# Two attention layers on one core: layer 0's weight pairs folded into one matrix each

The kernel runs on one core of a Trainium2 chip. The metric is the device time of one execution in microseconds; lower is better.

## The reference, cut to what matters

```python
# layer 0, 8 images of 1024 tokens, 256 channels, 4 heads, float32
qkv = einsum('bnc,cd->bnd', xf, W_qkv)            # q, k, v of each head: 256 wide
atten = softmax(einsum('bihd,bjhd->bijh', q, k) * C ** -0.5, axis=2)
res = einsum('bijh,bjhd->bihd', atten, v)
x1 = einsum('bnd,dc->bnc', res.reshape(B, -1, h * C), W_out) + b_out + xf
# layer 1: one head, keys 32 wide
b = softmax(einsum('bik,bjk->bij', x1 @ Wg + bg, x1 @ Wf + bf), axis=-1)
y = gamma * einsum('bij,bjd->bid', b, x1 @ Wh + bh) + x1
```

Per head, q k^T = x (Wq Wk^T) x^T, and (p v) Wo = p (x (Wv Wo)). Each bracket is a 256x256 product that doesn't depend on the image.

## The kernel before

```python
class Layer0:
    def prepare(self):                      # once per image and head
        for dst, col0 in ((self.q, 0), (self.k, C)):
            project_T(dst, w, col0, C, xT, ...)          # q^T and k^T, 16 instructions each
        project_rows(self.v, w, 2 * C, xT, ...)
    def rhs(self, c, k):
        return self.k[:, c, ts(k, NB)]
    def values(self, blk, pT):              # once per block of four query tiles
        for d in range(CC):
            ...                             # pav: 8 products of 128x512 over the keys
            nc.scalar.copy(res[:, d, :], pm)
        return lambda: self.project_out(blk, res)        # runs one step later
    def project_out(self, blk, res):
        for c in range(CC):
            ...                             # po: 2 products of 128x512 with W_out
            nc.vector.tensor_tensor(acc, pm, acc, ALU.add)   # acc: layer 0's output x1T

def scores(a, n, t):                        # one query tile
    ...                                     # s = q k^T, 128x1024 in PSUM
    nc.vector.tensor_reduce(nmax, s, AX.X, ALU.max, negate=True)
    if a.scale != 1.0:
        nc.vector.tensor_scalar(nbias, nmax, a.scale, None, ALU.mult)
    nc.scalar.activation(p, s, AF.Exp, bias=nbias, scale=a.scale, accum_out=psum)
    nc.vector.reciprocal(rsum, psum)
    a.after_softmax(t, p, rsum)             # layer 0: p *= rsum on VectorE
# ... cut: transposes of p (pp) into pT, layer 1, order of the work
        for t in range(NT):                 # per step of one query tile
            if nxt is not None and t == NT - 1 and i + 1 < len(order) - 1:
                nxt.prepare()
            p = scores(a, step, t)
            advance()     # transposes of the previous tile, then products that are due
```

## Time and profile before

| | kernel before |
|---|---|
| median of the runs beside the changed kernel | 3490.9 us (3484.8 to 3494.0, 4 runs) |
| span of the profiled run, granted TensorE clock | 3481.9 us, 0.992 |
| busy: TensorE, VectorE, ScalarE | 99%, 33%, 23% |
| TensorE instructions for k and for the output projection | 512 and 512 |
| steps whose transposes wait for the softmax | 71, by 0.20 us each |

The last row is my count over the whole list of TensorE's work in order of time: steps of layer 0 in which the transposes begin more than 0.1 us later than the eight score instructions need (8 x 0.4293 us).

A busy share of 99% does not by itself say that TensorE works at its best rate, since the ends of matmuls are modelled: a score instruction has a mean of 592 ns here, while the next one starts after 429. The distance from one start to the next is what I take as an instruction's cost. The prediction shows those lines. In them PE is TensorE, PEld its weight loads, DVE VectorE, ACT ScalarE, SP SyncE; PSUM is the memory in which this kernel's TensorE results stand (its pools ps_m, ps_t and so on); the granted clock is the share of TensorE's full clock that the profile records; a filler is a product that TensorE does between the scores of one tile and those of the next while the softmax runs.

### The profile page before, as it was taken

Reading aid. Unit: us, or ns where it says so; the run is one execution under the profiler, and the core shown is the slowest. Engines: PE = TensorE matmul, PEld = TensorE weight load, DVE = VectorE, ACT = ScalarE, POOL = GpSimd, SP = SyncE. Lnnn points to the kernel's source line nnn. Section 1 sums busy time; section 2 is a strip of 40 time slices with the busy share of each in tenths; the row PEclk is TensorE's granted clock in tenths of the full one; section 3 lists DMA queues with packets and bytes.
Section 4 is the critical chain, followed back from the end, with each engine's and each line's share of the span. In section 5 each row is a group of like instructions: output and inputs, shape, how many; then the busy total and the mean of one; then the engine's idle time right before and its main releaser. Section 6 shows DMA issues by size and latency. Waiting matters only on the chain.

```text
span 3481.9 us, 26369 instructions
## 1 busy us (share of the span) xinstructions
PE 3460.6 (99%) x11136; PEld 1856.9 (53%) x11136; DVE 1143.7 (33%) x2016; ACT 796.4 (23%) x1345; POOL 0.7 (0%) x6
## 2 busy tenths in 40 slices
PE   9999999999999999999999999999999999999999
PEld 4555555555555555555555454554545555555545
DVE  3333333333333333333333333333333333333333
ACT  2222222222222222222222222222222222222222
POOL 0000000000000000000000000000000000000000
PEclk9999999999999999999999999999999999999999
DMA  2000000000000000000000000000000000000000
GB/s 78 0 0 13 0 7 6 0 13 0 7 6 0 13 0 7 7 0 13 0 7 6 0 13 1 6 7 0 13 1 6 6 1 0 0 6 6 1 1 12
DMA packets 8341, 23.11 MB, mean 7 GB/s; under 512 B 1696, under 2 KB 3104, under 8 KB 8224
## 3 DMA queue, kind: packets, MB, share of 16 engines
q1 hardware_dynamic: 7136, 18.29, 1.5%
q10 hardware_dynamic: 1088, 3.15, 0.2%
q8 instruction: 88, 1.44, 0.2%
q14 instruction: 29, 0.24, 0.0%
HBM read 13.04 MB, written 8.39 MB: 6 GB/s over the span
## 4 chain that ended last, share of the span: by engine, by line
PE 99%; DVE 1%; ACT 0%; DMA 0%; issue 0%; SPq 0%; ACTq 0%
PE s L313 29%; PE pav L204 25%; PE pp L339 9%; PE py L294 6%; PE pm_q L139 6%; PE pr_v L155 6%; PE po L219 6%; PE pm_k L139 6%; PE pr_hv L155 2%; PE pm_f L139 1%; PE pm_g L139 1%; PE px L127 0%; PE px L267 0%; DVE nmax L321 0%; ACT p L329 0%; DMA x<-in_x_dram 0%
## 5 line engine op out<-in xcount | busy, mean ns | idle before, releaser
L313 PE MATMUL s<-k,q 128*128 128x512 f32 x2048 | 924.3, 592 | 0.0
L204 PE MATMUL pav<-pT,v 128*128 128x512 f32 x2048 | 893.9, 594 | 0.0
L321 DVE TENSOR_REDUCE nmax<-s 128x1 f32<-128x1024 f32 x320 | 391.9, 1225 | 1217.5 <-PE s L313 1208.4
L204 PEld LDWEIGHTS pav<-pT,v 128*128 128x128 f32 x2048 | 386.3, 191 | 462.0 <-issue 461.7
L313 PEld LDWEIGHTS s<-k,q 128*128 128x128 f32 x2048 | 376.4, 190 | 398.1 <-issue 396.3
L118 ACT COPY pT<-pp 128x512 f32<-128x512 f32 x320 | 187.6, 586 | 1091.6 <-PE pp L339 1091.6
L339 PEld LDWEIGHTS pp<-ident,p 128*128 128x128 f32 x2560 | 294.1, 143 | 213.3 <-issue 191.1
L339 PE MATMUL pp<-ident,p 128*128 128x128 f32 x2560 | 347.2, 280 | 7.0 <-DVE p L196 3.5
L329 ACT ACTIVATE p<-s,nbias 128x1024 f32<-128x1024 f32 x256 | 285.4, 1115 | 121.4 <-DVE nbias L324 121.4
L211 ACT COPY res<-pav 128x512 f32<-128x512 f32 x128 | 75.0, 586 | 715.3 <-PE pav L204 715.3
L219 PE MATMUL po<-res,wout_sb 128*128 128x512 f32 x512 | 230.4, 593 | 0.0
L294 PE MATMUL py<-hv,pT 128*128 128x256 f32 x1024 | 227.0, 381 | 0.0
L139 PE MATMUL pm_q<-xT,wqkv 128*128 128x512 f32 x512 | 227.0, 596 | 0.0
L155 PE MATMUL pr_v<-wqkv,xT 128*128 128x256 f32 x1024 | 226.2, 379 | 0.0
L139 PE MATMUL pm_k<-xT,wqkv 128*128 128x512 f32 x512 | 224.9, 592 | 0.0
L116 DVE COPY pT<-pp 128x512 f32<-128x512 f32 x320 | 218.0, 681 | 17.0 <-PE pp L339 17.0
L155 PEld LDWEIGHTS pr_v<-wqkv,xT 128*128 128x128 f32 x1024 | 194.6, 190 | 40.1 <-issue 15.3
L294 PEld LDWEIGHTS py<-hv,pT 128*128 128x128 f32 x1024 | 192.6, 190 | 33.4 <-issue 8.3
L196 DVE TENSOR_SCALAR p<-p,rsum 128x1024 f32<-128x1024 f32 x256 | 192.8, 753 | 9.0
L139 PEld LDWEIGHTS pm_k<-xT,wqkv 128*128 128x128 f32 x512 | 97.3, 190 | 122.5 <-issue 122.5
L139 PEld LDWEIGHTS pm_q<-xT,wqkv 128*128 128x128 f32 x512 | 97.4, 192 | 118.7 <-issue 109.6
L331 DVE RECIPROCAL rsum<-psum 128x1 f32<-128x1 f32 x320 | 52.0, 163 | 290.5 <-ACT p L329 290.5
(41 smaller groups left out, 1156.7 us busy)
## 6 DMA issues: line engine op xcount, KB each, us to landing
x<-in_x_dram SPq DMA_DIRECT2D x16, 512.0 KB, 4.4
out_dram<-y SPq DMA_DIRECT2D x16, 512.0 KB, 2.6
wqkv<-in_L_conv_W_qkv_dram ACTq DMA_DIRECT2D x4, 768.0 KB, 8.9
wout_sb<-in_L_conv_W_out_dram SPq DMA_DIRECT2D x1, 1024.0 KB, 15.1
wh_sb<-in_L_conv_Wh_dram SPq DMA_DIRECT2D x1, 256.0 KB, 10.2
bh_sb<-in_L_conv_bh_dram SPq DMA_DIRECT2D x1, 128.0 KB, 4.0
wf_sb<-in_L_conv_Wf_dram SPq DMA_DIRECT2D x1, 32.0 KB, 14.9
wg_sb<-in_L_conv_Wg_dram SPq DMA_DIRECT2D x1, 32.0 KB, 12.4
```

The source lines that it names most:

```text
L116: nc.vector.tensor_copy(dst, src)
L118: nc.scalar.copy(dst, src)
L139: nc.tensor.matmul(pm[:m], lhsT=w[:, c, col0 + d * P : col0 + d * P + m], rhs=src[:, c, ts(k, NB)], start=(c == 0), stop=(c == CC - 1),)
L155: nc.tensor.matmul(pm[:, ts(j, C)], lhsT=src[:, c, ts(2 * t2 + j, P)], rhs=w[:, c, col0 : col0 + C], start=(c == 0), stop=(c == CC - 1),)
L196: nc.vector.tensor_scalar(p, p, rsum, None, ALU.mult)
L204: nc.tensor.matmul(pm, lhsT=self.v[:, j, ts(d, P)], rhs=pT[:, j, :], start=(j == 0), stop=(j == NT - 1),)
L219: nc.tensor.matmul(pm, lhsT=wout_sb[:, h * CC + d, ts(c, P)], rhs=res[:, d, :], start=(d == 0), stop=(d == CC - 1),)
L294: nc.tensor.matmul(pm[:, :C], lhsT=pT[:, j, ts(ti, P)], rhs=self.hv[:, j, :], start=(j == 0), stop=(j == NT - 1),)
L313: nc.tensor.matmul(s[:, ts(k, NB)], lhsT=a.lhsT(c, t), rhs=a.rhs(c, k), start=(c == 0), stop=(c == a.kchunks - 1),)
L321: nc.vector.tensor_reduce(nmax, s, AX.X, ALU.max, negate=True)
L329: nc.scalar.activation(p, s, AF.Exp, bias=nbias, scale=a.scale, accum_out=psum)
L339: nc.tensor.transpose(pt[:, ts(j, P)], p[:, ts(g * HT + j, P)], ident)
```

## The change

The intent: k and the output projection are computed for every image and head. Folding the weights replaces them by two small products per head, done once on chip. The scores then take x^T itself in the place of k, and the value product lands directly in layer 0's output.

```diff
+    def fold_weights(h):                    # 12 transposes, 8 products of 128x256
+        for j in range(3):                  # Wq, Wk, Wv of the head, transposed
+            ...
+            copy_on(j, t.rearrange("p d c -> p (d c)"), pt)
+        for key, dst, lhs, rhs in (
+            ("wa", wa_sb, wT[0], wT[1]), ("wm", wm_sb, wT[2], wout_sb[h])
+        ):
+            ...
+            copy_on(h, t.rearrange("p c d -> p (c d)"), pm)
@@ Layer0.prepare
+            if h not in wa_sb:
+                fold_weights(h)
-            for dst, col0 in ((self.q, 0), (self.k, C)):
-                project_T(dst, w, col0, C, xT, ...)
+            project_T(self.q, wa_sb[h], 0, C, xT, ...)
-                self.v, w, 2 * C, xT,
+                self.v, wm_sb[h], 0, xT,
@@ Layer0.rhs
-            return self.k[:, c, ts(k, NB)]
+            return self.xT[:, c, ts(k, NB)]
@@ Layer0.values
-                nc.scalar.copy(res[:, d, :], pm)
-            return lambda: self.project_out(blk, res)
-        def project_out(self, blk, res): ...             # the po products
                 acc = x1T_of[b][:, c, ts(blk, NB)]
                 nc.vector.tensor_tensor(acc, pm, acc, ALU.add)   # pm is now pav
```

Cut: W_out is loaded in four pieces, and comments went, which moves line numbers.

More of the change, by code (lines that the diff above doesn't have):

```diff
@@ L85 @@
     wqkv_sb = []
+    wout_sb = []
+    wout_v = w_out.rearrange("(h k p) c -> h p k c", p=P, k=CC)
     for h in range(HEADS):
@@ L89 @@
         wqkv_sb.append(t)
-    wout_sb = const.tile([P, HEADS * CC, C], F32, tag="wout", name="wout_sb")
-    nc.sync.dma_start(wout_sb, w_out.rearrange("(k p) c -> p k c", p=P))
+        t = const.tile([P, CC, C], F32, tag=f"wout{h}", name=f"wout{h}")
+        nc.sync.dma_start(t, wout_v[h])
+        wout_sb.append(t)
     wf_sb = const.tile([P, CC, CK], F32, tag="wf", name="wf_sb")
@@ L118, in copy_on @@
             nc.scalar.copy(dst, src)
+    wa_sb, wm_sb = {}, {}
+    def fold_weights(h):
+        w = wqkv_sb[h]
+        wT = []
+        for j in range(3):
+            t = sb2.tile([P, CC, C], F32, tag="wT", name=f"wT_{h}_{j}", bufs=3)
+            pt = ps_t.tile([P, NB], F32, tag="pt", name=f"pw_{h}_{j}")
+            for d in range(CC):
+                for c in range(CC):
+                    nc.tensor.transpose(
+                        pt[:, d * C + c * P : d * C + (c + 1) * P],
+                        w[:, c, j * C + d * P : j * C + (d + 1) * P],
+                        ident,
+                    )
+            copy_on(j, t.rearrange("p d c -> p (d c)"), pt)
+            wT.append(t)
+        for key, dst, lhs, rhs in (
+            ("wa", wa_sb, wT[0], wT[1]), ("wm", wm_sb, wT[2], wout_sb[h])
+        ):
+            t = const.tile([P, CC, C], F32, tag=f"{key}{h}", name=f"{key}{h}")
+            pm = ps_m.tile([P, NB], F32, tag="pm", name=f"p{key}_{h}")
+            for c in range(CC):
+                for d in range(CC):
+                    nc.tensor.matmul(
+                        pm[:, ts(c, C)],
+                        lhsT=lhs[:, d, ts(c, P)],
+                        rhs=rhs[:, d, :],
+                        start=(d == 0),
+                        stop=(d == CC - 1),
+                    )
+            copy_on(h, t.rearrange("p c d -> p (c d)"), pm)
+            dst[h] = t
     def transpose_x(b):
@@ L170, in prepare @@
             b, h = self.b, self.h
-            xT, w = xT_of[b], wqkv_sb[h]
+            self.xT = xT = xT_of[b]
+            if h not in wa_sb:
+                fold_weights(h)
             self.q = sb2.tile([P, CC, N], F32, tag="q", name=f"q_{b}_{h}")
-            self.k = sb2.tile([P, CC, N], F32, tag="k", name=f"k_{b}_{h}")
             self.v = sb2.tile([P, NT, C], F32, tag="v", name=f"v_{b}_{h}")
-            for dst, col0 in ((self.q, 0), (self.k, C)):
-                project_T(
-                    dst, w, col0, C, xT,
-                    lambda i, d, k, pm: copy_on(i, dst[:, d, ts(k, NB)], pm),
-                )
+            project_T(
+                self.q, wa_sb[h], 0, C, xT,
+                lambda i, d, k, pm: copy_on(i, self.q[:, d, ts(k, NB)], pm),
+            )
             project_rows(
-                self.v, w, 2 * C, xT,
+                self.v, wm_sb[h], 0, xT,
                 lambda t2, pm: copy_on(
@@ L198, in values @@
         def values(self, blk, pT):
-            res = sb2.tile([P, CC, NB], F32, tag="res", name=f"res_{self.b}_{self.h}_{blk}")
-            for d in range(CC):
-                pm = ps_m.tile([P, NB], F32, tag="pm", name=f"pav_{self.b}_{self.h}_{blk}_{d}")
+            b, h = self.b, self.h
+            for c in range(CC):
+                pm = ps_m.tile([P, NB], F32, tag="pm", name=f"pav_{b}_{h}_{blk}_{c}")
                 for j in range(NT):
@@ L205, in values @@
                         pm,
-                        lhsT=self.v[:, j, ts(d, P)],
+                        lhsT=self.v[:, j, ts(c, P)],
                         rhs=pT[:, j, :],
@@ L209, in values @@
                         stop=(j == NT - 1),
-                    )
-                nc.scalar.copy(res[:, d, :], pm)
-            return lambda: self.project_out(blk, res)
-        def project_out(self, blk, res):
-            b, h = self.b, self.h
-            for c in range(CC):
-                pm = ps_m.tile([P, NB], F32, tag="pm", name=f"po_{b}_{h}_{blk}_{c}")
-                for d in range(CC):
-                    nc.tensor.matmul(
-                        pm,
-                        lhsT=wout_sb[:, h * CC + d, ts(c, P)],
-                        rhs=res[:, d, :],
-                        start=(d == 0),
-                        stop=(d == CC - 1),
                     )
```

## The prediction

> **What bounds the kernel now.** I read first the page's top (busy times and the chain that ended last), then the groups by line, then the order of time of one engine. Of the slices, PE stands at 9 tenths in all 40, and the granted clock is 0.992.
>
> ```profile
> PE 3460.6 (99%) x11136; PEld 1856.9 (53%) x11136; DVE 1143.7 (33%) x2016; ACT 796.4 (23%) x1345; POOL 0.7 (0%) x6
> ...
> PE 99%; DVE 1%; ACT 0%; DMA 0%; issue 0%; SPq 0%; ACTq 0%
> ```
>
> TensorE is busy 99% of the span and 99% of the chain that ended last is its own work; VectorE works a third of the time and ScalarE a quarter. So what is taken off TensorE comes off the time, as long as no wait grows in its place. The groups say what there is to take:
>
> ```profile
> L219 PE MATMUL po<-res,wout_sb 128*128 128x512 f32 x512 | 230.4, 593 | 0.0
> L139 PE MATMUL pm_k<-xT,wqkv 128*128 128x512 f32 x512 | 224.9, 592 | 0.0
> L211 ACT COPY res<-pav 128x512 f32<-128x512 f32 x128 | 75.0, 586 | 715.3 <-PE pav L204 715.3
> L339 PE MATMUL pp<-ident,p 128*128 128x128 f32 x2560 | 347.2, 280 | 7.0 <-DVE p L196 3.5 <-ACT p L329 0.9
> ```
>
> The x512 is a count of instructions, then come busy time and the mean of one: the program asks for 256 products with k (8 images, 4 heads, 2x2 output tiles, 2 contraction chunks), the profile shows 512, so each fp32 product is two instructions. The busy times of the groups may not be added up as gains: each group's last matmul has a modelled tail that lies over the next group's start (all PE groups together give 3593 us, more than the span). What an instruction is worth is read from the starts in order of time:
>
> ```profile
> 1053.97 3.60 PE L313 MATMUL s<-k,q 128*128 128x512 f32 x8
> 1057.40 1.04 PE L339 MATMUL pp<-ident,p 128*128 128x128 f32 x8
> 1058.28 3.60 PE L313 MATMUL s<-k,q 128*128 128x512 f32 x8
> 1061.92 1.06 PE L339 MATMUL pp<-ident,p 128*128 128x128 f32 x8
> 1062.82 3.60 PE L313 MATMUL s<-k,q 128*128 128x512 f32 x8
> 1066.26 1.04 PE L339 MATMUL pp<-ident,p 128*128 128x128 f32 x8
> 1067.13 13.90 PE L204 MATMUL pav<-pT,v 128*128 128x512 f32 x32
> 1080.87 3.60 PE L313 MATMUL s<-k,q 128*128 128x512 f32 x8
> 1084.30 1.04 PE L339 MATMUL pp<-ident,p 128*128 128x128 f32 x8
> 1085.17 3.60 PE L219 MATMUL po<-res,wout_sb 128*128 128x512 f32 x8
> 1088.61 3.60 PE L313 MATMUL s<-k,q 128*128 128x512 f32 x8
> ```
>
> This is one block of four query tiles of layer 0. Eight score instructions take 3.43 us from start to start (0.429 us each), eight transposes 0.875 us (0.109 each), the 32 of the value product 13.74 us, the eight of the output projection 3.44 us. In all but one place the next row starts when the last has had its own time: scores at 1058.28 to transposes at 1061.92 is 3.64 us, 0.21 too much. There the transposes wait for the softmax of the tile before. VectorE shows why:
>
> ```profile
> 1057.61 1.22 DVE L321 TENSOR_REDUCE nmax<-s 128x1 f32<-128x1024 f32 x1 [4.47 <-PE s L313]
> ...
> 1061.02 0.75 DVE L196 TENSOR_SCALAR p<-p,rsum 128x1024 f32<-128x1024 f32 x1
> ```
>
> The softmax of a tile takes from 1057.40 (scores done) to 1061.77 (p scaled), 4.4 us with the hop to TensorE about 4.5; a step without other products gives it 0.875 + 3.43 = 4.31 us. So the kernel is bound by TensorE, but steps without a filler product are 0.2 us from being bound by the softmax. Where such steps follow each other, the delay of one gives the next its slack, and only every second one shows it.
>
> [...] a dropped fp32 product of 128x512 is worth 0.859 us. [...] the mean here is 280, but the spacing is 109 ns, and the spacing is what I use. [...] after TensorE's one wait of 3.48 us (at 3379 us) the same eight transposes take 1.81 us from start to start. [...]
>
> **The change part by part.**
>
> Removed on TensorE: 512 instructions for k and 512 for the output projection, 1024 x 0.4293 us = 439.6 us. All of it lies on the path: the timeline shows k as 6.87 us per head between q and v, and the output projection as 3.44 us per block with no wait around it.
>
> Removed elsewhere: the copies of k (44.3 us VectorE, 37.5 ScalarE) and the res copies (75.0 ScalarE). These engines are off the path, so this is worth nothing by itself.
>
> Moved: the value product now makes layer 0's output, and VectorE adds it to x1T straight from PSUM, with the same additions (0.69 and 0.75 us) that served the output projection. One falls in the middle of the 13.74 us value product and one at its end, where VectorE has been idle for nearly 14 us. No cost. The scores read xT in place of k, with the same shapes: no cost. xT has two buffers, and the next image's is written near the end of head 3 into the one of the image before: no new wait.
>
> Added, once per head, in the first image: 12 transposes, 12 x 0.109 = 1.3 us, and 8 products of 128x256, which are 16 instructions at 0.216 us (32 of pr_v take 6.90 us) = 3.45 us. That is 4.75 us, four times 19 us. Around them are waits: the transposes want the two PSUM buffers that the probabilities' transposes are just leaving, their copies stand in the queues of VectorE and ScalarE among the softmax of the tile just scored (4.4 us), and the product needs both copies. Laid over the softmax times above, I get some 7 us for a fold in heads 1 to 3 and 5 for the first, where q must follow a transpose, a copy, a product and a copy: 26 us in all (an estimate from these durations).
>
> Lost cover: 32 of the 64 blocks of layer 0 go from the output projection straight to scores (in the others the projections of the next head follow and cover still). There three steps without filler follow each other, not two, and the delay of 0.21 us shows twice in place of once: 32 x 0.21 = 7 us. Layer 1's steps are shorter (1.9 us scores, 0.95 transposes) and one block of layer 0 ends among them per image. Its output projection at 918.94 covers a softmax that is ready at 920.8; without it the transposes would come at 920.85. So nearly nothing, I set 2 us in all.
>
> Sum for the span: 3481.9 - 439.6 + 26 + 7 + 2 = 3077.3 us. The median time is 8.7 us above the profiled span (3490.6 against 3481.9): 3086 us, 11.6% less.
>
> **The rivals.**
>
> First: the softmax takes the place of the work removed. For it: the 4.5 us against 4.31, and the filler that goes is just what loosened this loop. Against it: the loop is short by 0.2 us only, and the value product of 13.74 us resets it in every block. If each of the steps without filler paid (3 x 64 x 0.21 = 40 us against some 13 now) and layer 1 lost 1 us in each image, the time would be 3086 - 9 + 27 + 8 = 3112 us.
>
> Second: VectorE becomes a stop. The addition that frees the value product's PSUM buffer is now in VectorE's queue, in order with the softmax; ScalarE, which was free then, did it before. If the additions hold up a softmax, a block would lose up to 0.7 us, 45 us in all: 3131 us. Against it: 33% busy, and idle before the first maximum after the value product.
>
> Third: the whole busy time counts. 230.4 + 224.9 = 455.3 us off and 19 on, no waits: 3054 us. Against it: the spacing of 0.429 us, which leaves 439.6 to be had.
>
> Fourth: the fold is dear at the start. The weights for the first image come at about 400 GB/s until 16 us, and wout took 15.1 us to land; the first fold may wait for its piece of it, which is now the third load of its queue. That would be up to 7 us more: 3093 us.
>
> **Range and chances.** The sum's large term is exact to 1 or 2 us. The fold may be 20 to 45 us, the lost cover 0 to 30. The three runs before spread by 6 us. That gives 3068 to 3108. To miss 2% the waits would have to give back 370 of 440 us, for which nothing in the profile speaks; I leave 1% each for that and for a program that is slower.
>
> **What would show the steps right or wrong.** The groups po, pm_k and res are gone, the others of layer 0 keep their counts, and new groups with 48 transposes and 64 instructions of 128x256 (16 per head) appear in the first image only. Score instructions stay at 0.429 us from start to start. PE stays at 98 to 99% of the span, with the chain on it. Blocks in the middle of a head shrink from 34.64 to about 31.4 us, heads by another 6.87. In them the delay of 0.21 us shows twice. The fold's stretch in heads 1 to 3 is 5 to 10 us. I am wrong if the mean of score instructions changes (then xT is not like k as an operand), if transposes wait over 0.5 us in each step (first rival), or if the value product waits for an addition (second).

The sum in it came to 3077.3 us for the span (3481.9 - 439.6 + 26 + 7 + 2) and 3086 us for the time. The 439.6 us come from the spacing in the trace, 0.4293 us. The 280 and 109 ns are those of a transpose (pp).

## The result, and the profile after

| | before | after |
|---|---|---|
| median | 3490.9 us | 3074.6 us (3070.5 to 3079.6, 4 runs) |
| ratio | 1 | 0.8812 (0.8797 to 0.8827) |
| span of the profiled run, clock | 3481.9 us, 0.992 | 3068.7 us, 0.991 |
| TensorE instructions | 11136 | 10224 |
| steps whose transposes wait for the softmax | 71 x 0.20 us | 96 x 0.20 us |

Ratios in this text are the mean time of one kernel's fast runs over that of the other's of the same rounds, so not quite the ratio of the medians. All runs told of here were fast (within 1.5% of the fastest run of the same kernel). The prediction was 3086 us, between 3068 and 3108.

Top of the page and chain of the changed kernel (shares of the span):

```profile
PE 3044.6 (99%) x10224; PEld 1680.0 (55%) x10224; DVE 1111.1 (36%) x1964; ACT 687.2 (22%) x1161; POOL 0.7 (0%) x6
...
PE 98%; DVE 1%; ACT 0%; DMA 0%; issue 0%; ACTq 0%
```

Nothing took TensorE's place: 912 instructions are gone, 1024 taken off and 112 added for the folds, and the chain is still its own work. The groups of the changed kernel (busy us, mean ns of one, idle before):

```profile
L340 PE MATMUL s<-xT,q 128*128 128x512 f32 x2048 | 925.4, 592 | 0.0
L366 PE MATMUL pp<-ident,p 128*128 128x128 f32 x2560 | 347.8, 280 | 7.8 <-DVE p L238 3.2 <-ACT p L356 0.9
L260 DVE TENSOR_TENSOR x1T<-pav,x1T 128x512 f32<-128x512 f32 x96 | 66.4, 691 | 478.2 <-PE pav L246 478.2
L152 PE MATMUL pwa<-wT,wT 128*128 128x256 f32 x32 | 8.7, 421 | 0.0
L138 PE MATMUL pw<-ident,wqkv 128*128 128x128 f32 x48 | 8.0, 313 | 1.1 <-ACT xT L125 1.1
```

The mean of a score instruction is 592 ns with xT as operand, as it was with k. VectorE waits 478 us in all for the value product before its additions: it is there in time. The value product doesn't wait for it: its line on the page (L246) has 0.0 us idle before it. Nor does the addition hold up the softmax in the block below; it ends at 154.60 us, 2.7 us before the scores of the next maximum are done:

```profile
153.91 0.69 DVE L260 TENSOR_TENSOR x1T<-pav,x1T 128x512 f32<-128x512 f32 x1 [6.17 <-PE pav L246]
157.34 1.22 DVE L348 TENSOR_REDUCE nmax<-s 128x1 f32<-128x1024 f32 x1 [2.74 <-PE s L340]
```

A block in the middle of a head, TensorE in order of time (start, duration), to be laid beside the block in the prediction:

```profile
122.27 3.60 PE L340 MATMUL s<-xT,q 128*128 128x512 f32 x8
125.70 1.04 PE L366 MATMUL pp<-ident,p 128*128 128x128 f32 x8
126.58 3.60 PE L340 MATMUL s<-xT,q 128*128 128x512 f32 x8
130.22 1.06 PE L366 MATMUL pp<-ident,p 128*128 128x128 f32 x8
131.12 3.60 PE L340 MATMUL s<-xT,q 128*128 128x512 f32 x8
134.56 1.04 PE L366 MATMUL pp<-ident,p 128*128 128x128 f32 x8
135.43 3.60 PE L340 MATMUL s<-xT,q 128*128 128x512 f32 x8
139.07 1.06 PE L366 MATMUL pp<-ident,p 128*128 128x128 f32 x8
139.97 13.90 PE L246 MATMUL pav<-pT,v 128*128 128x512 f32 x32
153.71 3.60 PE L340 MATMUL s<-xT,q 128*128 128x512 f32 x8
```

The block takes 31.44 us (122.27 to 153.71) where it took 34.64. The output projection's 3.44 us are gone, and one more wait has come: from scores to transposes it is 3.64 us at 126.58 and again at 135.43. Over the whole trace there are 25 more such waits, 5 us.

A fold, that of head 1, in the same view:

```profile
76.73 1.02 PE L340 MATMUL s<-xT,q 128*128 128x512 f32 x2
77.59 1.07 PE L138 MATMUL pw<-ident,wqkv 128*128 128x128 f32 x8
78.49 1.02 PE L340 MATMUL s<-xT,q 128*128 128x512 f32 x2
79.36 0.60 PE L138 MATMUL pw<-ident,wqkv 128*128 128x128 f32 x4
79.79 1.97 PE L152 MATMUL pwa<-wT,wT 128*128 128x256 f32 x8
81.59 1.89 PE L152 MATMUL pwm<-wout,wT 128*128 128x256 f32 x8
83.32 7.03 PE L181 MATMUL pm_q<-xT,wa 128*128 128x512 f32 x16
```

From 76.73 to 83.32 it is 6.59 us, of which four score instructions take 1.72: the fold costs 4.87 us, its own work and hardly any wait. Score instructions of the next tile were put between its transposes, just where I had counted waits. The first fold costs more: head 0's scores start at 33.31 us, against 32.82 before, although 6.87 us of k had gone from in front of them. That is 7.4 us, of which 4.75 are the fold's own work as the prediction costs it.

### The profile page after: what moved, and what is told of

It is laid out like the page before. It is cut to its first block, busy times and chain, and to the rows that moved or that the text cites. A ratio compares the mean times of both kernels' runs of the same rounds, so it can differ in the third digit from the quotient of the medians.

```text
span 3068.7 us, 24316 instructions
## 1 busy us (share of the span) xinstructions
PE 3044.6 (99%) x10224; PEld 1680.0 (55%) x10224; DVE 1111.1 (36%) x1964; ACT 687.2 (22%) x1161; POOL 0.7 (0%) x6
## 4 chain that ended last, share of the span: by engine, by line
PE 98%; DVE 1%; ACT 0%; DMA 0%; issue 0%; ACTq 0%
PE s L340 33%; PE pav L246 29%; PE pp L366 10%; PE py L321 7%; PE pr_v L197 7%; PE pm_q L181 7%; PE pr_hv L197 2%; PE pm_f L181 1%; PE pm_g L181 1%; PE px L294 0%; PE px L169 0%; DVE nmax L348 0%; ACT p L356 0%; DMA wqkv<-in_L_conv_W_qkv_dram 0%; PE pwa L152 0%; PE pw L138 0%
## 5 line engine op out<-in xcount | busy, mean ns | idle before, releaser
L340 PE MATMUL s<-xT,q 128*128 128x512 f32 x2048 | 925.4, 592 | 0.0
L246 PE MATMUL pav<-pT,v 128*128 128x512 f32 x2048 | 894.5, 595 | 0.0
L246 PEld LDWEIGHTS pav<-pT,v 128*128 128x128 f32 x2048 | 386.6, 191 | 462.4 <-issue 462.1
L340 PEld LDWEIGHTS s<-xT,q 128*128 128x128 f32 x2048 | 374.0, 190 | 383.3 <-issue 381.4
L260 DVE TENSOR_TENSOR x1T<-pav,x1T 128x512 f32<-128x512 f32 x96 | 66.4, 691 | 478.2 <-PE pav L246 478.2
L197 PE MATMUL pr_v<-wm,xT 128*128 128x256 f32 x1024 | 226.2, 379 | 0.0
L181 PE MATMUL pm_q<-xT,wa 128*128 128x512 f32 x512 | 225.0, 592 | 0.0
L197 PEld LDWEIGHTS pr_v<-wm,xT 128*128 128x128 f32 x1024 | 194.6, 190 | 40.1 <-issue 15.3
L181 PEld LDWEIGHTS pm_q<-xT,wa 128*128 128x128 f32 x512 | 95.1, 190 | 107.3 <-issue 93.7
L340 PE MATMUL s<-f,g 32*128 32x512 f32 x256 | 138.8, 659 | 3.4 <-ACT p L356 3.4
L123 DVE COPY v<-pr_v 128x512 f32<-128x512 f32 x64 | 44.3, 692 | 176.4 <-PE pr_v L197 176.4
L255 DVE SCALAR_TENSOR_TENSOR x1T<-pav,bout_sb,xT 128x512 f32<-128x512 f32 x32 | 24.0, 750 | 182.2 <-PE pav L246 182.2
```

What stands on the lines that cost most here:

```text
L123: nc.vector.tensor_copy(dst, src)
L181: nc.tensor.matmul(pm[:m], lhsT=w[:, c, col0 + d * P : col0 + d * P + m], rhs=src[:, c, ts(k, NB)], start=(c == 0), stop=(c == CC - 1),)
L197: nc.tensor.matmul(pm[:, ts(j, C)], lhsT=src[:, c, ts(2 * t2 + j, P)], rhs=w[:, c, col0 : col0 + C], start=(c == 0), stop=(c == CC - 1),)
L246: nc.tensor.matmul(pm, lhsT=self.v[:, j, ts(c, P)], rhs=pT[:, j, :], start=(j == 0), stop=(j == NT - 1),)
L340: nc.tensor.matmul(s[:, ts(k, NB)], lhsT=a.lhsT(c, t), rhs=a.rhs(c, k), start=(c == 0), stop=(c == a.kchunks - 1),)
```

## The experiments

My theory is the prediction's: TensorE's spacing is the price; the fold costs its own work; where the output projection goes, the softmax shows in one more step of a block. The rivals: the parts don't add up as costed; VectorE became a stop; the small waits are no waits for the softmax. Four runs went beside each other on one chip, then four, then three, each group beside the kernel before (medians 3486.8, 3486.8 and 3490.2 us). The changed kernel itself ran again only in the second group; comparisons with it from the other two go over groups.

**Fold Wq Wk^T only.** The output projection is put back.

```diff
-        for j in range(3):
+        for j in range(2):
-            ("wa", wa_sb, wT[0], wT[1]), ("wm", wm_sb, wT[2], wout_sb[h])
+            ("wa", wa_sb, wT[0], wT[1]),
-                self.v, wm_sb[h], 0, xT,
+                self.v, wqkv_sb[h], 2 * C, xT,
+    # values() and project_out() as in the kernel before
```

> Only Wq Wk^T is folded; v, the res copies and the output projection stay. My theory (TensorE's spacing is the price, 512 instructions x 0.429 us = 220 us off; per head 8 transposes and 16 instructions of 128x256, 0.88 + 1.73 us, four times about 11 us with the start on; the output projection still gives its 3.4 us of cover in each block, so the waits of transposes stay at about 71): about 3491 - 220 + 11 = 3282 us, ratio 0.940. If the cover that the output projection gave were unimportant, the whole change is just the sum of this run and the next; if k's products had hidden something, this run gains clearly less than 205 us. If busy time were the price: 3491 - 225 + 11 = 3277.

Measured: 3283.4 us, ratio 0.9411 (0.9386 to 0.9435), 71 waits.

**Fold Wv Wo only.** k is computed and read as before.

```diff
-        for j in range(3):                  # wT with 3 buffers
+        for j in (2,):                      # wT with 1 buffer
-            ("wa", wa_sb, wT[0], wT[1]), ("wm", wm_sb, wT[2], wout_sb[h])
+            ("wm", wm_sb, wT[2], wout_sb[h]),
+            # prepare() makes q and k from wqkv_sb[h]; rhs() returns self.k
```

> Only Wv Wo is folded; k is computed per image and read by the scores as before (one transposed-weight buffer instead of three, for room). My theory: 220 us off for the output projection, some 9 us on for the folds (4 transposes and 16 instructions of 128x256 per head, and their waits), and the lost cover: waits of transposes for the softmax in 95 or so steps instead of 71, 5 us. About 3285 us, ratio 0.941. Rival (VectorE becomes a stop when it frees the value product's PSUM): the value product or the scores after it wait, and the run is 20 to 45 us dearer than that.

Measured: 3285.0 us, ratio 0.9411 (0.9384 to 0.9438), 96 waits. The two parts save 5.9% each and 11.8% together, and the waits come with the output projection's part alone. Both are the prediction's costs. My range of error here is about 5 us (the runs spread by 6 to 12), so the 225 us of the busy time against the 220 of the spacing are not told apart by these two alone. Both runs also bear 6 to 7 us at the start: the scores of the first head begin at 33.18 us (k is gone) and 39.05 us (k stays), against 32.82, although each has only half the fold.

**Fold for every image.** The fold's cost times eight.

```diff
-            if h not in wa_sb:
-                fold_weights(h)
+            fold_weights(b, h)
```

> The changed kernel with the fold done again for every image, 28 folds more. My estimate in the prediction was 7 us a fold with waits; the trace of the changed kernel shows in heads 1 to 3 about 4.9 us between the rows around it, its own work and no wait. So 28 x 4.9 = 137 us more than the changed kernel: about 3212 us, ratio 0.920. If the prediction's 7 us were right: 28 x 7 = 196 us, 3271 us, ratio 0.937.

Measured: 3221.5 us, ratio 0.9228 (0.9199 to 0.9256): about 146 us over the changed kernel, 5.2 us for each of 28 folds. The prediction's 7 us per fold is refuted; the folds in the trace look like that of head 1 above. Some of the 146 us is the clock: the stretches at a lowered clock cost 39.5 us in this trace and 27.4 in the changed kernel's. Without them the two spans differ by 138.6 us, 4.95 us a fold.

**ScalarE takes the value product out of PSUM.**

```diff
+                res = sb2.tile([P, NB], F32, tag="res", ...)
+                nc.scalar.copy(res, pm)
+                pm = res
                 acc = x1T_of[b][:, c, ts(blk, NB)]
```

> The changed kernel, but ScalarE copies the value product out of PSUM (as it did before the change) and VectorE adds from the copy. Second rival (VectorE holds the PSUM buffer too long or holds up the softmax): this is faster than the changed kernel, by up to 45 us. My theory (it is idle there): same as the changed kernel within its spread of 5 us, ratio 0.881.

Measured: 3076.5 us, ratio 0.8812, as the changed kernel. Who empties the value product's buffers is of no account here. The other half of the second rival, an addition that holds up a softmax, is not tested by this run, since VectorE still adds; the two VectorE lines under the result speak against it. With both the second rival falls.

**The scale in the fold.** The softmax gets one VectorE step shorter. 1/16 is a power of two. The outputs are right.

```diff
+            if key == "wa":
+                nc.vector.tensor_scalar(t..., pm, SCALE, None, ALU.mult)
+            else:
                 copy_on(h, t.rearrange("p c d -> p (c d)"), pm)
-            self.b, self.h, self.scale = b, h, SCALE
+            self.b, self.h, self.scale = b, h, 1.0      # nbias is then nmax itself
```

> The changed kernel with the scale 1/16 multiplied into the folded query weights, so that the step nmax -> nbias on VectorE is gone (about 0.24 us from the end of one to the start of the next). My theory of the waits: the softmax takes 4.5 us against 4.31 us of TensorE work in a step without filler; with 0.24 us less it fits, the 96 waits of 0.205 us before transposes vanish and TensorE goes straight from scores to transposes: 96 x 0.23 = 20 to 22 us less than the changed kernel, ratio to it 0.993. If the 0.2 us were a fixed cost of TensorE (a switch from scores to transposes) and no wait for the softmax, nothing changes.

Beside it ran the changed kernel once more, as reference:

> The changed kernel itself, as the reference for the three runs beside it: ratio 0.881, 3070 to 3080 us.

Measured: the reference 3076.4 us, ratio 0.8822 (0.8810 to 0.8834), 96 waits; with the scale in the fold 3044.6 us, ratio 0.8734 (0.8723 to 0.8746), none of the 96 waits left. TensorE in order of time, the same place in a block as above:

```profile
126.42 3.60 PE L343 MATMUL s<-xT,q 128*128 128x512 f32 x8
129.86 1.04 PE L369 MATMUL pp<-ident,p 128*128 128x128 f32 x8
130.73 3.60 PE L343 MATMUL s<-xT,q 128*128 128x512 f32 x8
134.17 1.04 PE L369 MATMUL pp<-ident,p 128*128 128x128 f32 x8
```

Scores to transposes is 3.44 us in every step. So the 0.2 us were a wait for the softmax and not a cost of TensorE. The gain of the medians is 32 us, 10 more than expected. Runs at the same granted clock differ by less: at 0.991 the changed kernel took 3070.5 and 3071.7 (in the first session), this one 3044.6, some 26 us. The rest is the clock, below. With the lowered stretches taken out of both traces it is 24.6 us: 19 are the waits, nearly 3 the rows of transposes behind them, 2 layer 1's first wait. The edit may also have taken more out of the softmax than the expected 0.24 us. In the changed kernel's trace, from the start of a tile's maximum to the end of p's scaling is 4.16 us (125.91 to 130.07). In it the maximum is done at 127.14; nbias starts only at 127.64, behind a copy of 0.68 us in VectorE's queue, and ScalarE starts at 127.88. Without nbias the softmax no longer waits for that copy, which would be up to 0.7 us (an estimate from these times).

**The softmax one step longer.**

```diff
-            nc.vector.tensor_scalar(nbias, nmax, a.scale, None, ALU.mult)
+            nc.vector.tensor_scalar(half, nmax, 2.0 * a.scale, None, ALU.mult)
+            nc.vector.tensor_scalar(nbias, half, 0.5, None, ALU.mult)
```

> The changed kernel with one more VectorE step of the same kind in the softmax (scale by 2/16, then by 1/2), about 0.24 us longer. My theory: the same 96 steps or a few more wait 0.44 us in place of 0.205: 22 to 30 us more than the changed kernel, ratio to it 1.008. If every step without filler paid (first rival), 2 x 96 x 0.24 = 46 us more. If the wait is a fixed cost of TensorE: nothing changes.

Measured: 3105.8 us, ratio 0.8904 (0.8892 to 0.8916), to the reference 1.009. There are 94 waits of 0.39 us on average (17 us more in all, from my count); in the first of a block:

```profile
126.58 3.60 PE L340 MATMUL s<-xT,q 128*128 128x512 f32 x8
130.41 1.06 PE L368 MATMUL pp<-ident,p 128*128 128x128 f32 x8 [0.23 <-DVE p L238]
```

The wait is now 0.39 us, part of it long enough to show as idle time behind p. Only every second step pays, as before (in all blocks but one), so the first rival falls too: it had every step pay. The other 12 of 29 us go largely with a lower clock (0.986 in all runs, 0.988 to 0.990 in the reference's).

**Layer 1's value projection later.** This came from the trace, not from the change: in layer 1's first steps the granted clock falls.

```diff
-            project_rows(self.hv, wh_sb, 0, x1T, add_bias)
+            self.late = {0: lambda: project_rows(..., range(half)),
+                         1: lambda: project_rows(..., range(half, 2 * half))}
             p = scores(a, step, t)
+            if isinstance(a, Layer1) and t in a.late:
+                a.late.pop(t)()
```

> The changed kernel with layer 1's value projection (7 us of full-size TensorE work) moved from before its scores to behind the first two score tiles. The trace shows that layer 1's first steps, with half their work transposes and scores of 32 rows, often run at a lower granted clock for 3 to 7 us (in 5 of 7 images and at the end). If this comes from too little work of TensorE in that stretch, the stretches keep the full clock, the wait of 0.49 us there goes, and the time falls by 10 to 25 us, the spread between runs with it. If it comes from something else, the time stays within 5 us.

Measured: 3041.4 us, ratio 0.8720 (0.8708 to 0.8732); its four runs lie within 1.6 us, where the reference's spread by 7. One stretch of layer 1 in the changed kernel and in this one (stretch and its length; busy time of the engines with counts; then granted clock, DMA share, GB/s):

```profile
419.00:429.00 10.00, 9.51 (x27) 4.87 (x26) 5.51 (x11) 4.69 (x8) 0.00 (x0) 0.71 0.00 0
```

```profile
419.00:429.00 10.00, 10.00 (x37) 6.16 (x37) 3.97 (x9) 2.30 (x4) 0.00 (x0) 1.00 0.00 0
```

The wait of 0.49 us and the clock of 0.71 are both gone. The 0.71 is an average over the stretch. A narrower window of the changed kernel's trace shows half the clock for some 6.8 us:

```profile
423.30:430.00 6.70, 6.70 (x20) 4.16 (x20) 2.87 (x7) 2.48 (x6) 0.00 (x0) 0.50 0.00 0
```

Added over such stretches, the clock below full cost the changed kernel's profiled run about 27 us (length times the missing half), this one's 4 us; the waits of 0.49 us in seven images are 3 us more. That is most of the 28.5 us between the two spans (3068.7 and 3040.2). The rest of the 35 us between the medians goes with the reference's lower clock (0.988 to 0.990, against 0.991 in that profiled run). The edit changes two things at once, the wait and the mix of work, so it doesn't say which of them lowered the clock.

**The same move in the kernel before.**

> The kernel before with only layer 1's value projection moved. The lowered clock costs the kernel before about as much (29 us summed over its slow stretches in the trace, against 27 in the changed kernel), so it has nothing to do with the fold: about 35 us less than before, 3452 us, ratio 0.990, clock 0.998 or more. The fold's own gain, this run against the changed kernel with the same move (3041), should then again be about 411 us. If the fold had made the clock worse or better, this gains clearly less or more than 35.

The edit is the same. Measured: 3451.5 us, ratio 0.9891 (0.9876 to 0.9906), clock 1.000, four runs within 0.6 us. So the clock is no noticeable part of what the fold did: 3451.5 - 3041.4 = 410 us, as without the move (3486.8 - 3076.4 = 410). The 3041.4 is from the group before, on another chip, and the first measurement gave 416, so this holds to some 6 us.

**Both that gained.**

> Both changes that gained together: the scale in the fold and layer 1's value projection later. If they act on different places (waits of transposes in layer 0; clock and waits in layer 1), the gains add but for what each took of the 0.49 us wait and the clock: 3041 - 22 = 3019 us, between 3012 and 3025, ratio 0.866. If both won the same thing, about 3040.

Measured: 3018.6 us, ratio 0.8650 (0.8637 to 0.8663), correct, four runs within 1.1 us. It is the fastest kernel, 1.8% faster than the changed one by the ratios (0.8650 / 0.8812).

**The transposes of x1 later.** What lowers the clock, too little full-size work or the wait?

```diff
+            def x1_tiles():
                 for t2 in range(NT // 2):
                     ...                      # 16 transposes and their copies, as they were
+            self.late = {3: x1_tiles}
```

> The changed kernel with layer 1's 16 transposes of x1 moved from before its first score tiles to its fourth, where then s, x1 transposes and p transposes follow each other for about 15 us with no full-size product between. If stretches of transposes and 32-row scores, with next to no idle time, lower the clock, the drops move there or add there, and the time is 5 to 25 us over the changed kernel's 3075. If the wait of 0.49 us (which stays where it was) is what lowers it, the drops stay at 418 to 430 us of an image and none comes at the new place.

Measured: 3087.5 us, ratio 0.8853 (0.8837 to 0.8869), 11 to 14 us over the changed kernel by its two ratios. But the drops did not come where I expected them. Two stretches of layer 1 of the second image, the old place behind the short wait and the new place:

```profile
797.00:807.00 10.00, 10.00 (x28) 5.27 (x28) 2.87 (x7) 2.60 (x6) 0.00 (x0) 0.66 0.00 0
817.00:832.00 15.00, 15.00 (x71) 8.68 (x71) 10.11 (x17) 7.59 (x13) 0.00 (x0) 1.00 0.01 1
```

From 817.3 to 830.5 us there are only transposes and 32-row scores, 13 us of them, then layer 1's value product; all of it ran at the full clock (1.00 from 817 to 832). The stretch after the wait of 0.49 us (at 795 us) fell. But the wait alone isn't it either: in the first image the same instructions with the same wait (at 419.5 us) kept the full clock (1.00 from 410 to 440 us). The time had risen because the old place dropped in six images of seven, not five, and the clock in the last image's tail was at half for longer (some 31 us by slices of 10 us, against 13.7 in the changed kernel).

## Why the prediction was right, step by step

1. **What bounds the kernel** held: TensorE 99%, then 99%; its chain 99%, then 98%.
2. **The price of an instruction**, 0.429 us, held. From the start of eight score instructions to the next row is 3.43 us before (1053.97 to 1057.40) and after (122.27 to 125.70). The two parts alone saved 5.9% each and came within 2 us of my 3282 and 3285 us. In that is some luck: the kernel before was 4 us faster beside them than the 3491 that I had reckoned from, and the saving was 203 and 202 us where I had 209 and 206. The whole change decides it better. The lowered clock cost the two profiled runs 29.0 and 27.4 us; without it the spans differ by 411.6 us. The costs of points 4 and 5, 22 and 5 us, put back on that, give 439: the 439.6 of the spacing and not the 455.3 of the third rival.
3. **xT in the place of k, additions from PSUM by VectorE: no cost.** Held. The mean of a score instruction stayed at 592 ns, and taking the additions' PSUM reading away changed nothing (3076.5 us against 3074.6 and 3076.4).
4. **The fold, 26 us, was 22.** The split was further off than the sum: 5 + 21 was predicted, 7.4 + 14.6 measured. In heads 1 to 3 score instructions filled the waits. In head 0 nothing could. Fold and q waited for the start's copies, as the fourth rival had it in kind. But it wasn't W_out that came late: ScalarE made its first copy at 11.70 us, after its table load at 10.41 us, which stood behind its issue of the weights' loads. That issue took 9.64 us, against 6.63 before, and the table load came 3.0 us later for it. The run with the fold for every image, also with four loads of W_out, has its table load at 10.7 us, and in all eleven traces with four loads the fold's first transposes, which such a copy released, begin at 12.25 to 12.65 us (12.34 in the changed kernel). So part of the first fold's 7.4 us may go with the split of W_out, which came with this change; no run splits W_out without a fold, or folds without the split.
5. **The lost cover, 7 us, was 5**: 25 more waits of 0.2 us, not 32. Counted block by block, 25 of the 32 got one wait more, those with the next image's transposes too. The other seven lie among layer 1's steps, one in each image from the second, and kept the three waits that they had; I had counted them here and under layer 1. That it is the softmax was shown by shortening and by lengthening it.
6. **Layer 1, 2 us.** With the lowered clock taken out as in point 2, about 1 us is left over for it.
7. **8.7 us from span to time** was a wrong term. Every run takes 1.7 to 1.9 us longer than its own span. The rest of the 8.7 us was the difference between the profiled run and the median run, and in the changed kernel that was 4 us.

Terms 4 to 7 were too large by some 4, 2, 2 and 3 us, which is the 11 us between 3086 and 3074.6. All four err on the same side; the last is partly chance, since it hangs on which run was profiled. The second and third rival would have given 3131 and 3054 us; both lie outside the measured runs.

One thing the prediction did not see: 71 waits of 0.2 us and the lowered clock, mostly in layer 1, were in the kernel before, 14 and 29 us. The second went there by a small move; the first was removed only in the changed kernel, and no run tried it in the kernel before. The prediction read the first and took it for given; the second hid behind a mean clock of 0.992. It looked only at the one wait of 3.48 us, behind which the clock is at half for some 3.4 us (3382.9 to 3386.3). The same trace has half the clock for 10.2 us in four other places (at 465, 1328, 2192 and 3055 us), each behind a wait of only 0.49 us.

## What to carry to other kernels

If one engine is busy throughout, cost a change by the distance between starts of its instructions (439.6 us here) and not by the busy time of a group (455.3), and then ask what the removed work was covering. Compare the softmax's (or any chain's) length with the work between its start and its use: here 4.5 us stood against 4.31, and taking one small VectorE step out of the chain, a factor that could be folded into a weight, gave back about as much as the whole folding cost (25 us against 22). A mean clock just under one can hide stretches at half of it (0.991 here, with 0.50 from 423.3 to 430.0 us); look at the clock in slices of a few microseconds, and see whether runs that spread differ in it.

## What the traces show of the clock and of the transposes

- The clock was at half (0.50 from 423.3 to 430.0 us in the changed kernel) behind a wait of 0.49 us (and still behind 0.22 us, at 420 us, when the scale was in the fold) among transposes and 32-row scores. In the runs without the moved value projection this came in three to six of seven images; in the traces before and after it lasted 6.8 or 10.2 us. The changed kernel's 96 waits of 0.2 us among full-size scores lie in none of its lowered stretches, nor did the clock fall in 13 us of such narrow work without a wait (1.00 from 817 to 832 us with the transposes of x1 later). What exactly sets it off is not settled by these runs. With seven more microseconds of full-size work in that place, and without the wait, no such stretch was lowered (every slice of 10 us before 2940 us at 0.99 or more; 4 us lost in the whole trace).
- The lowered stretches lie in the middle of the kernel, and differences from run to run went with the mean clock: the kernel before took 3483.5 us at a mean clock of 0.992 and 3493.3 at 0.989; with the clock at 1.000 four runs lay within 0.6 us.
- The duration of a transpose is 280 ns, but eight in a row start 109 ns apart (226 ns where the clock was halved: 1.81 us from 3382.92 us in the kernel before), and the granted clock stayed at 1.00 for 13 us where transposes and narrow scores were all that ran. Transposes alone were not tried.
- A 128x128 by 128x512 product in float32 is two instructions here, 0.859 us.
